# Half-width products in two chunks' scores of a graph network, and an earlier planned landing for the first gathered rows

## The chip, the cores and the metric

The kernel runs on one core of one Trainium2 chip. The metric is the device time of one execution in microseconds (us); of the kernel before, three runs are shown. The five engines of the core are named as the profile names them: PE (TensorE, with PEld for its weight loads), DVE (VectorE), ACT (ScalarE), POOL (GpSimd) and SP (SyncE, which here only issues transfers).

## What is computed

The graph has 2708 nodes with 512 features each, and a dense 0/1 adjacency matrix. Four layers follow each other, each with a residual connection and a layer norm. Layers 0, 1 and 3 are products of the adjacency with the features and a weight matrix. Layer 2, where the change lies, is two attention layers over all pairs of nodes:

```python
def _gat_layer(x, W, adj):
    proj = x @ W
    Wh, Ws = jnp.split(proj, 2, axis=-1)
    scores = Wh @ Ws.T
    a = jax.nn.softmax(scores, axis=-1) * adj
    out = a @ Wh
    out = out + x
    return jax.nn.leaky_relu(out, NEG_SLOPE)
```

The softmax runs over all 2708 nodes, and is masked by the adjacency only afterwards. So all scores are needed for the maximum and the sum, but after the mask some 16 of 2708 weights in a row are left.

## The kernel before

**Tiling.** Nodes are cut into 22 blocks of 128 (the last has 20) and, as columns, into six chunks `CH` of 512, 512, 512, 512, 384 and 276. Scores are kept turned: the score tile of block j and chunk k has block j's nodes on the partitions and chunk k's nodes in the columns.

**One attention layer** (`Attention`, from line 1385) works so. `project_steps` (line 1491) makes, for each chunk, the weights of the scores `wst` (four tiles of 128 features by the chunk's nodes) and the projected rows `z`, which go to a table `pairs` in memory. Then `layer` (line 1827) walks the chunks. For each it runs `scores` (line 1552) for blocks 0, 1, 2, 21, 3, 4 up to 20: four float32 products of 128x128 weights with 512 moving columns add up in a PSUM bank, and ACT copies the bank to a tile `s`. The hardware runs each float32 product as two instructions. Block 21, with 20 rows, puts its four products beside each other on the array (`few`, line 673), and DVE adds them up. `greatest` (line 1578) keeps the running maximum `top` of the score tiles.

**Softening.** While the scores of chunk k are made, the chunk before, k-1, is finished. `shift_rows` (line 1586) transposes `top` on PE (`tr_top`), reduces it on DVE and spreads the result, `shift_columns` (line 1607) transposes it back (`tr_mx`), and ACT copies it out. Then `soften` (line 1623) takes one block at a time: DVE subtracts the maximum, ACT takes the exponential, DVE adds to the running sum, DVE multiplies by the mask, and SP stores the block to the table `pairs`. The step of block v subtracts and exponentiates block v, and sums, masks and stores block v-1. One or two steps are recorded per block of scores. All masks of a chunk are loaded at the start of the next.

**Gathering and weighing.** When a chunk's last block is softened, `fetch` (line 1677) has POOL issue indirect transfers: each gathers, for a list of 128 neighbours, a row of the table that holds both the weights and the neighbours' `z`. Up to ten are under way. `weigh` (line 1732) multiplies such a list on PE into a bank `acc`. A block of 128 nodes takes four single lists and eight narrow ones, of which four run side by side, so a full chunk has 48 lists. There are two tables `pairs` for a layer, used in turn. `end` (line 1768) divides, adds the residual and applies the leaky relu.

**The order.** Each engine's order of instructions is that in which the program records them: `Ordered` (line 54) ties each instruction to the one before it on its engine. The program records by a clock of its own: `advance` (line 1722) adds the planned time of each product, and `weigh` takes a list when its planned landing has passed. The planned landing is set in `fetch`, lines 1697 to 1699: the lists follow each other by 1.15 us and land 6 us later, and a chunk's first begins 16 us after it is recorded. PE follows this order strictly; where a list is not there in time, it stands still. Where the walk is over, `until` and the loops behind it fill in the next layer's work (`second`, line 1902, or `early`, line 605), and `need` (line 1890) takes lists without looking at the clock where the next layer wants the rows.

**Memory.** Almost all tiles are pages of 128x512 float32 from one pool of 82; gathered lists lie in 11 wider ones. PSUM has eight banks in two halves of four: scores take theirs from half 0, transposes, sums and `acc` from half 1. `index` (line 1200) makes the lists of neighbours from marks that `note` (line 838) takes while layer 1 reads the adjacency, with tiles in a pool of its own.

Of the kernel before, what the change touches and what calls it, by code (L numbers as in the profile page):

```python
# [19 lines left out]
P = 128  # L20
# [22 lines left out]
PAGES, WIDES = 82, 11  # L43
# [44 lines left out]
class Kernel:  # L88


    def __init__(self, ctx, tc, x_in, x_t, adj, adj_t, w0, b0, w1, b1, w2, w2_t, w3, b3, out):
        self.tc, self.nc = tc, tc.nc
        nc = self.nc
        self.ctx = ctx
        self.x_in, self.x_t, self.adj, self.adj_t, self.out = x_in, x_t, adj, adj_t, out
        self.w0, self.b0, self.w1, self.b1, self.w2 = w0, b0, w1, b1, w2
        self.w2_t, self.w3, self.b3 = w2_t, w3, b3
        const = ctx.enter_context(tc.tile_pool(name="const", bufs=1))
        self.small = ctx.enter_context(tc.tile_pool(name="small", bufs=4))
        scratch = ctx.enter_context(tc.tile_pool(name="scratch", bufs=1, space=DRAM))  # L100
        tile_ = lambda name, shape, dt: const.tile(shape, dt, tag=name, name=name)
        self.ident = tile_("ident", [P, P], FP)
        self.ones = tile_("ones", [P, P], FP)
        self.ones_b = tile_("ones_b", [P, P], BF)

        self.rdeg = tile_("rdeg", [P, NB], FP)
        self.dis = tile_("dis", [P, NB], FP)
        self.nbad = len(CH) * NB
        self.bad = tile_("bad", [P, self.nbad + NB], FP)


        self.feeds = tile_("feeds", [P, NB, QUARTERS, NB], BF)
        self.givers = tile_("givers", [P, NB, LISTS], I32)

        self.base = tile_("base", [P, QUARTERS], FP)
        self.upto = tile_("upto", [P, P], BF)
        self.node = tile_("node", [P, 1], FP)
        self.block = tile_("block", [P, NB], BF)
        self.since = tile_("since", [P, P], BF)
        self.saved = [  # L120
            [scratch.tile([P, D], FP, tag=f"x{s}_{i}", name=f"x{s}_{i}") for i in range(NB)]
            for s in range(3)
        ]
        self.between = [
            scratch.tile([P, D], FP, tag=f"y_{i}", name=f"y_{i}") for i in range(NB)
        ]

        self.masks = [
            scratch.tile([P, NB, w], U8, tag=f"mask{k}", name=f"mask{k}")
            for k, (_, w) in enumerate(CH)  # L130
        ]

        self.turned = [
            [
                scratch.tile([P, DC, w], FP, tag=f"t{s}_{k}", name=f"t{s}_{k}")
                for k, (_, w) in enumerate(CH)
            ]
            for s in range(2)
        ]

    def constants(self, page):
# [4 lines left out]
        nc.gpsimd.memset(self.feeds, 0.0)  # L146
# [313 lines left out]
    def other_weights(self):  # L460


        nc = self.nc
        with self.tc.tile_pool(name="ps_bad", bufs=1, space=PSUM) as ps_bad:
            total = self.small.tile([P, 1], FP, tag="bad_sum", name="bad_sum")
            nc.vector.tensor_reduce(total, self.bad, AX.X, ALU.add)
            ps = ps_bad.tile([P, 1], FP, tag="bad", name="bad_ps")
            nc.tensor.matmul(ps, self.ones, total, start=True, stop=True)
            flag = self.small.tile([P, 1], I32, tag="flag", name="flag")
            nc.vector.tensor_scalar_min(flag, ps, 1.0)  # L470
        return nc.values_load(flag[0:1, 0:1])


def blocks_of(k):

    c0, cw = CH[k]
    return [(c0 // P + q, q * P, min(P, cw - q * P)) for q in range(-(-cw // P))]

# [37 lines left out]
class Fast:  # L516
# [4 lines left out]
    def __init__(self, kernel):  # L521
        self.k, self.tc = kernel, kernel.tc
        self.nc = Ordered(kernel.tc)
        self.notes = []
# [10 lines left out]
    def run(self):  # L535
        kernel, nc = self.k, self.nc
        with ExitStack() as ctx:
# [4 lines left out]
            self.small, self.lists = pool("small_f", 4), pool("lists", 1)  # L542
# [295 lines left out]
    def note(self, k, g, at):  # L838

        (c0, cw), (j0, j1) = CH[k], GROUPS[g]  # L840
        feeds = self.k.feeds.rearrange("p i q j -> p j (i q)")
        i0, full = c0 // QW, cw // QW
        sets = [(j0, j1, P)] if j1 < NB else [(j0, j1 - 1, P), (j1 - 1, j1, QW)]
        for q0, q1, n in ((0, full, QW), (full, -(-cw // QW), cw % QW)):
            for a, b, rows in sets if q0 < q1 else ():
                v = at[:rows, a - j0 : b - j0, q0 * QW : q0 * QW + (q1 - q0) * n]
                self.nc.vector.tensor_reduce(
                    feeds[:rows, a:b, i0 + q0 : i0 + q1],
# [351 lines left out]
    def index(self, k):  # L1200
# [8 lines left out]
        tile_ = lambda tag, shape, dt: self.lists.tile(shape, dt, tag=tag, name=f"{tag}{k}")  # L1209
# [31 lines left out]
        f = kernel.feeds[:, i0 : i0 + n, :, :]  # L1241
        nc.vector.tensor_scalar(f, f, 0.0, None, ALU.not_equal)
        some, a, b = (tile_(t, one, BF) for t in ("some", "a", "b"))
# [13 lines left out]
        kept = tile_("kept", one, BF)  # L1257
# [26 lines left out]
        def examine():  # L1284

            top = tile_("top", [P, n], FP)
# [13 lines left out]
        row, which = tile_("row", one, BF), tile_("which", one, BF)  # L1300
# [5 lines left out]
        sums = tile_("sums", [P, n, 2 * LISTS], FP)  # L1306
# [16 lines left out]
        t = tile_("list", [P, n, LISTS], FP)  # L1323
# [5 lines left out]
    def one_hot(self, s, row, which):  # L1329
# [12 lines left out]
        tile_ = lambda tag, w: self.lists.tile([P, NB, w], BF, tag=tag, name=f"{tag}{s}", bufs=2)  # L1342
        hit, both = tile_("hit", LISTS), tile_("both", 2 * LISTS)
# [13 lines left out]
class Chunk:  # L1357


    def __init__(self, ly, k):  # L1360
# [3 lines left out]
        self.s, self.masks, self.ends = {}, {}, []  # L1364
        self.softened = 0
        self.fetched, self.rden = [], None
# [12 lines left out]
class AttentionLayer:  # L1379
    def __init__(self, number, pairs):  # L1380
        self.number, self.pairs = number, pairs
        self.w, self.mixed, self.xt, self.wst = [], [], {}, {}


class Attention:
# [7 lines left out]
    def __init__(self, fast):  # L1393
# [16 lines left out]
        self.mixed = self.scratch.tile([DC, P, D], FP, tag="mixed", name="mixed")  # L1410
        self.layers = [AttentionLayer(a, self.pairs[a]) for a in range(2)]
        self.clock, self.fetch_free, self.pending = 0.0, 0.0, []

# [77 lines left out]
    def project_steps(self, ly, k):  # L1491
# [4 lines left out]
        for m in range(DC):  # L1496
# [13 lines left out]
            yield True  # L1510
        for i, lo, n in blocks_of(k):
# [29 lines left out]

    def load_moving(self, ch):
# [9 lines left out]
    def scores(self, ch, j):  # L1552
# [6 lines left out]
        if n <= QW:  # L1559
            ps = self.f.few(  # L1560
                0, name, n, cw, lambda c: wst[c][:, lo : lo + n], lambda c: ch.xt[c][:, :cw]
            )
            self.f.total(s[:n, :cw], ps, n, cw)
            self.advance(cost(cw))
# [10 lines left out]
        nc.scalar.copy(s[:n, :cw], ps[:n, :cw])  # L1575
        self.advance(DC * cost(cw))

    def greatest(self, ch, j):
        n, cw, s = rows_of(j), ch.cw, ch.s[j]
        if j == 1:  # L1580
            ch.top = self.page(f"top{ch.name}")
            self.nc.vector.tensor_max(ch.top[:, :cw], ch.s[0][:, :cw], s[:, :cw])
        elif j > 1:
            self.nc.vector.tensor_max(ch.top[:n, :cw], ch.top[:n, :cw], s[:n, :cw])
# [31 lines left out]
    def load_masks(self, ch):  # L1616
        for j0, j1 in GROUPS:
            a = self.page(f"a{ch.name}_{j0}", U8, (P, DC, ch.cw))
            self.nc.sync.dma_start(a[:, : j1 - j0, :], self.k.masks[ch.k][:, j0:j1, :])
            for j in range(j0, j1):  # L1620
                ch.masks[j] = a[:, j - j0, :]

    def soften(self, ch):
# [4 lines left out]
        if v < NB:  # L1628
            if v == 0 and ch.k >= 2:

                assert not self.chunks[ch.k - 2].to_fetch
            n = rows_of(v)
            s = ch.s[v][:n, :cw]
            nc.vector.tensor_sub(s, s, ch.shift[:n, :cw])
            nc.scalar.activation(s, s, AF.Exp)
        j = v - 1
        if j < 0:
            return
        n = rows_of(j)
# [37 lines left out]
    def fetch(self, ch):  # L1677
# [19 lines left out]
        begin = max(self.fetch_free, self.clock + (16 if (q, t) == ch.first_fetch else 0))  # L1697
# [3 lines left out]
    def load_rows(self, ch, q):  # L1701
# [7 lines left out]
        if ch.ly.number == 1:  # L1709
            ch.first[q] = self.page(f"x1{ch.name}_{q}")  # L1710
            self.nc.sync.dma_start(ch.first[q][:w], self.k.saved[1][i][:w])

    def fetch_ahead(self):
        count = sum(len(c.fetched) for c in self.chunks)
        for c in self.chunks:
            while c.to_fetch:
                if c.softened <= NB or count >= self.AHEAD:
                    return
# [13 lines left out]
    def weigh(self, wait=False):  # L1732
# [16 lines left out]
        if first:  # L1749
            ch.acc = self.bank(1, f"acc{ch.name}_{q}")  # L1750
        for h, g in enumerate(gs):
# [74 lines left out]

    def layer(self, ly, chunks, fill):
        f = self.f
        self.chunks, self.made = chunks, {}
        for k, ch in enumerate(chunks):  # L1830
            old = chunks[k - 1] if k else None


            js = [0, 1, 2, NB - 1, *range(3, NB - 1)]
            for n, j in enumerate(js):
                if old and n == 0:
                    self.load_masks(old)
                if old and n >= 3:
                    if n == 3 and k >= 3:
                        while chunks[k - 3].to_weigh:  # L1840
                            self.weigh(True)
                    for _ in range(1 + n % 2):
                        if old.softened <= NB:
                            self.soften(old)
                self.scores(ch, j)
# [3 lines left out]
                if n == 4 and k + 1 < len(chunks):  # L1849
                    self.load_moving(chunks[k + 1])  # L1850
                if k + 1 == len(chunks) and n in ((5, 11, 19) if ly.number == 0 else (5, 11)):
                    next(fill)
                if old and n == 0:
                    self.greatest(old, js[-1])
                if n:
                    self.greatest(ch, js[n - 1])
# [4 lines left out]
                if old and n == 1:  # L1861
                    self.shift_rows(old)
                if old and n == 2:
                    self.shift_columns(old)
        last = chunks[-1]
        self.load_masks(last)
        self.greatest(last, js[-1])
# [7 lines left out]

        done = self.clock + (2 if ly.number == 0 else 4)
        while last.softened <= NB:
# [108 lines left out]
```

## Time and profile before

| what | us |
|---|---|
| median of three runs | 2330.78 |
| lowest and highest run | 2322.93 to 2333.93 |
| the profiled execution: span, from its first to its last instruction | 2297.7 |
| PE busy in the span | 2269.4 |
| DVE, POOL, ACT busy | 1391.5, 705.4, 675.5 |
| scores of the first attention layer, first to last product | 760.2 to 1249.1 |
| scores of the second attention layer | 1456.2 to 1939.7 |

The profiled execution gives a span and no time of its own beside it; the difference of the median run to this span is 33.1 us. A row of a group reads: line, engine, operation, tile written, tiles read, shape and count, then the busy time and the mean of one in ns, then the idle time of the engine just before these instructions and what ended it. All instructions carry line 71, where `Ordered` issues them, so they are told apart by the names of their tiles: `sp` are the scores, `acc<-g` the products with gathered lists, `acc<-m` those of the adjacency layers. A row of the timeline reads: start, time from the first start to the last end, engine, operation, count, and in brackets the idle time before it. A row of stretches gives, behind its bounds and length, the busy time of PE, PEld, DVE, ACT and POOL with their counts, then the clock granted to PE, the busy share of the DMA engines and GB/s.

### The profile page before, as it was taken

The page shows a single profiled execution, that of the slowest core. Times are in us where ns is not written, and L with a number is a line of the kernel's source. Part 1 is how long each engine was busy: PE and PEld are TensorE (multiplying, and loading weights), DVE is VectorE, ACT ScalarE, POOL GpSimd, SP SyncE. Part 2 cuts the span into 40 slices and gives each one's busy share as a digit, 9 for nine tenths or more (in the row PEclk, how much of TensorE's full clock was granted, in tenths as well). Part 3 has the DMA queues.
Part 4 walks back from the last instruction along what each step waited for, and adds up shares of the span by engine and source line. Part 5 has one row for each costly group of instructions (what it writes and reads, how often), then busy time and mean ns, then how long its engine had stood idle before and what let it go on. Part 6 is the DMA issues. An engine that isn't in the chain of part 4 may idle for free.

```text
span 2297.7 us, 25903 instructions
## 1 busy us (share of the span) xinstructions
PE 2269.4 (99%) x8525; PEld 1289.0 (56%) x8525; DVE 1391.5 (61%) x2803; ACT 675.5 (29%) x1354; POOL 705.4 (31%) x822
## 2 busy tenths in 40 slices
PE   9999999999999999999999999999999999899997
PEld 6776876777644444443555444444443555466685
DVE  6777787786553537748667511238769788525523
ACT  7444452322111123223322200113223334342211
POOL 3433431111000001635557540001635467442000
PEclk9999999999999999999999999999999999999999
DMA  9966752223547415858789997405868799963311
GB/s 351 286 188 184 199 168 81 76 81 104 208 184 267 144 25 184 303 191 297 254 311 360 349 412 284 183 8 179 303 218 286 254 322 339 334 217 120 116 51 43
DMA packets 260929, 486.34 MB, mean 212 GB/s; under 512 B 40238, under 2 KB 126950, under 8 KB 260784
## 3 DMA queue, kind: packets, MB, share of 16 engines
q1 hardware_dynamic: 192128, 269.63, 33.6%
q0 software_dynamic: 68656, 214.96, 28.0%
q8 instruction: 69, 1.13, 0.2%
q14 instruction: 76, 0.62, 0.1%
HBM read 307.55 MB, written 176.92 MB: 211 GB/s over the span
## 4 chain that ended last, share of the span: by engine, by line
PE 86%; DMA 6%; DVE 4%; ACT 1%; issue 1%; POOL 1%; SPq 0%; ACTq 0%; POOLq 0%; DVEq 0%
PE sp L71 33%; PE acc L71 30%; PE mm L71 8%; PE z L71 6%; PE wst L71 6%; DMA x<-x 2%; DMA x<-in_x 1%; DMA at<-in_adj_t 1%; DMA g<-pairs,givers 1%; PE mix L71 1%; DMA pairs<-s 1%; POOL xt L71 1%; PE list L71 1%; ACT m L71 1%; PE tr_x2t L71 0%
## 5 line engine op out<-in xcount | busy, mean ns | idle before, releaser
L71 PE MATMUL sp<-xs,wst_sb 128*128 128x512 f32 (+3 forms) x2112 | 798.3, 544 | 0.0
L71 POOL DMA_INDIRECT g<-pairs,givers x510 | 524.2, 1028 | 872.9 <-issue 338.9
L71 PEld LDWEIGHTS sp<-xs,wst_sb 128*128 128x128 f32 (+1 forms) x2112 | 379.7, 186 | 408.4 <-issue 324.8
L71 PE MATMUL acc<-m,xh 128*128 128x512 f32 (+4 forms) x1584 | 566.8, 379 | 6.6 <-ACT m L71 5.1
L71 PE MATMUL acc<-m,xl 128*128 128x512 f32 (+4 forms) x1584 | 549.6, 365 | 2.0 <-DVE xl L71 1.8
L71 PEld LDWEIGHTS acc<-m,xh 128*128 128x128 f32 (+1 forms) x1584 | 288.0, 188 | 70.9 <-issue 21.3
L71 PEld LDWEIGHTS acc<-m,xl 128*128 128x128 f32 (+1 forms) x1584 | 288.3, 188 | 46.3 <-issue 5.3
L71 PE MATMUL acc<-g 128*32 128x512 f32 (+1 forms) x1020 | 264.8, 606 | 4.6 <-DMA g<-pairs,givers 4.0
L71 ACT COPY s<-sp 128x512 f32<-128x512 f32 (+2 forms) x252 | 132.7, 528 | 396.8 <-PE sp L71 395.1
L71 ACT ACTIVATE s<-s 128x512 f32<-128x512 f32 (+3 forms) x264 | 151.6, 580 | 319.8 <-DVE s L71 319.5
L71 DVE TENSOR_TENSOR top<-top,s 128x512 f32<-128x512 f32 (+2 forms) x240 | 149.1, 621 | 156.1 <-ACT s L71 154.5
L71 PE MATMUL mm<-w,ht 128*128 128x512 f32 (+1 forms) x528 | 223.7, 593 | 0.0
L71 ACT CAST m<-at 128x512 fp32r<-128x512 uint8 (+5 forms) x396 | 199.2, 567 | 62.3 <-DMA at<-mask 19.7
L71 DVE TENSOR_TENSOR s<-s,shift 128x512 f32<-128x512 f32 (+3 forms) x264 | 162.7, 620 | 36.2 <-ACT shift L71 36.2
L71 DVE TENSOR_TENSOR s<-s,a 128x512 f32<-128x512 f32 (+3 forms) x264 | 165.8, 628 | 13.6 <-DMA a<-mask 4.5
L71 DVE TENSOR_TENSOR sum<-sum,s 128x512 f32<-128x512 f32 (+4 forms) x252 | 156.5, 621 | 15.4 <-ACT s L71 15.4
L71 PEld LDWEIGHTS mm<-w,ht 128*128 128x128 f32 (+1 forms) x528 | 95.8, 186 | 117.0 <-issue 112.2
L71 PEld LDWEIGHTS acc<-g 128*32 128x32 f32 (+1 forms) x1020 | 74.6, 134 | 148.0 <-issue 116.5
L71 PE MATMUL z<-w,xt 128*128 128x512 f32 (+1 forms) x352 | 151.0, 596 | 0.0
L71 PE MATMUL wst<-xt,mixed 128*128 128x512 f32 (+2 forms) x384 | 150.5, 544 | 0.0
L71 POOL DMA_DIRECT2D x<-o x44 | 26.0, 597 | 329.7 <-DVE o L71 325.4
L71 PEld LDWEIGHTS wst<-xt,mixed 128*128 128x128 f32 x384 | 72.0, 190 | 71.1 <-issue 58.8
(168 smaller groups left out, 1476.7 us busy)
## 6 DMA issues: line engine op xcount, KB each, us to landing
pairs<-z_sb SPq DMA_DIRECT2D x84, 768.0 KB
pairs<-s SPq DMA_DIRECT2D x168, 256.0 KB
at<-in_adj_t SPq DMA_DIRECT2D x84, 256.0 KB
xres<-x POOLq DMA_DIRECT2D x44, 256.0 KB, 4.6
x<-o POOLq DMA_DIRECT2D x43, 256.0 KB, 3.4
pairs<-s SPq DMA_DIRECT2D x84, 128.0 KB
x<-x SPq DMA_DIRECT2D x37, 256.0 KB
at<-mask SPq DMA_DIRECT2D x32, 256.0 KB
```

The source lines that it names most:

```text
L71: ins = call(*args, **kw)
```

## The change

**Seven products for eight.** In chunks 0 and 1 of each attention layer (`SEVEN`), blocks are taken in ten pairs; blocks 18 and 21 stay alone. A pair of blocks, with the features in two halves and the columns in two halves, is a 2x2 product of quarter matrices. It took eight products of 256 columns (in the kernel before, four of 512 columns for each block, each over a quarter of the features). Winograd's form of Strassen's scheme takes seven, each over two quarters of the features, on sums of weights (s1 to s4) and of moving operands (t1 to t4). The seven are recorded interleaved over neighbouring pairs. Partial results stay in PSUM banks x and y and are copied out by ACT between additions; DVE adds what is left. The weight sums are made in `project_steps` (`sum_weights`), s3 takes the place of a quarter of the weights, which is saved to memory and restored during chunk 1, and the sums of the first four weight chunks are stored during chunk 0 and loaded again for chunk 1.

**Softening.** Subtraction, exponential and mask of a block are recorded one step apart (two in chunks 0 and 1) instead of in one or two steps. Chunks wait in a list; during chunk 1 one step is recorded at each half pair, and what is left goes on in chunk 2, with two steps a block while two chunks wait. Masks are loaded a group at a time. `shift_rows` and `shift_columns` come one block later in the walk, so between them lies block 21 and not block 2.

**The planned landing.** A chunk's first list begins 6 us of the program's clock after it is recorded, not 16.

**Beside these.** The marks of `note` and the tiles of `index` become pages, cleared a chunk at a time; the pool has 87 pages; the constant of ones becomes one column, and the final flag is summed with bfloat16 ones. The residual's second input is loaded when a block is first weighed.

```diff
-PAGES, WIDES = 82, 11
+PAGES, WIDES = 87, 11
...
+STREAMED = 4
+FIRST_LANDS = 6
+SOFT = NB + 2 * 2
+ALONE = 18
+SEVEN = [0, 1]
...
+    def sum_weights(self, ly, k):
...
+        for c in range(2):
+            nc.vector.tensor_add(tiles["s1"][c], a21[c], a22[c])
+            nc.vector.tensor_sub(tiles["s2"][c], tiles["s1"][c], a11[c])
+            nc.vector.tensor_sub(tiles["s4"][c], a12[c], tiles["s2"][c])
+            nc.sync.dma_start(self.quarter[ly.number][k][c], a21[c])
...
+    PRODUCTS = {
+        1: ("a11", "b11"),
+        2: ("a12", "b21"),
+        3: ("s4", "b22"),
+        4: ("a22", "t4"),
+        5: ("s1", "t1"),
+        6: ("s2", "t2"),
+        7: ("s3", "t3"),
+    }
+
+    def product(self, ch, t, n, out, start=False):
+
+        b, (w, x) = t["b"], self.PRODUCTS[n]
+        for c in range(2):
+            self.nc.tensor.matmul(
+                out,
+                t["sums"][w][c][:, bass.ts(b, P)],
+                ch.part[x][c],
+                start=(start and c == 0),
+                stop=(c == 1),
+                skip_group_check=not start,
+            )
+        self.advance(2 * cost(ch.half))
+
+    def pair_steps(self, ch):
...
+        def ahead(t):
+            self.product(ch, t, 2, t["y"][:, :h], start=True)
+            self.product(ch, t, 5, t["y"][:, h:cw], start=True)
+            nc.scalar.copy(t["r"][:, h:cw], t["y"][:, h:cw])
+
+        def one(t):
+            t["x"] = self.bank(t["n"] % 3 // 2, f"spx{t['name']}")[:, :h]
+            self.product(ch, t, 1, t["x"], start=True)
+            nc.scalar.copy(t["s"][:, :h], t["x"])
+
+        def six(t):
+            self.product(ch, t, 3, t["y"][:, h:cw])
+            self.product(ch, t, 6, t["x"])
+            nc.scalar.copy(t["s"][:, h:cw], t["x"])
+
+        def seven(t):
+            self.product(ch, t, 7, t["x"])
+            t["v"] = self.page(f"v{t['name']}")
+            nc.scalar.copy(t["v"][:, :h], t["x"])
+
+        def four(t):
+            self.product(ch, t, 4, t["x"])
+            nc.scalar.copy(t["r"][:, :h], t["x"])
+            ch.complete.append(t["j"][1])
+
+        def first_block(t):
+            nc.vector.tensor_add(t["s"][:, :cw], t["s"][:, :cw], t["y"][:, :cw])
+            ch.complete.append(t["j"][0])
+
+        def second_block(t):
+            nc.vector.tensor_add(t["r"][:, h:cw], t["r"][:, h:cw], t["v"][:, :h])
...
+            t = begin(n, p)
+            ahead(t)
+            if old:
+                first_block(old)
+            yield "mid"
+            one(t)
+            if older:
+                four(older)
+            if ch.k and p[1] == 0 and p[0] + 1 in groups:
+                self.load_sums(ch.ly, p[0] + 1)
...
+            yield "end"
+            if old:
+                seven(old)
+            yield "mid"
+            six(t)
+            if old:
+                second_block(old)
+            older, old = old, t
+            yield "end"
...
@@ -1626,16 +1894,23 @@
...
             nc.vector.tensor_sub(s, s, ch.shift[:n, :cw])
+        j = v - ch.apart
+        if 0 <= j < NB:
+            s = ch.s[j][: rows_of(j), :cw]
             nc.scalar.activation(s, s, AF.Exp)
-        j = v - 1
+        j -= ch.apart
         if j < 0:
             return
+        if j == NB - 1:
+            ch.softened = SOFT
...
-        begin = max(self.fetch_free, self.clock + (16 if (q, t) == ch.first_fetch else 0))
+        begin = max(self.fetch_free, self.clock + (FIRST_LANDS if (q, t) == ch.first_fetch else 0))
...
+            for what in self.walk(ch):
+                if what == "mid":
+                    self.soften_next()
+                    self.weigh()
+                    continue
+                n += 1
...
+                if old and n < 2:
+                    self.greatest(old, last=n == 1)
+                many = 2 if len(self.to_soften) > 1 else 1 + n % 2
+                for _ in range(0 if ch.seven else many):
+                    self.soften_next()
                 f.beat()
...
-                if old and n == 1:
+                if old and n == 2:
                     self.shift_rows(old)
-                if old and n == 2:
+                if old and n == 3:
                     self.shift_columns(old)
+                    self.to_soften.append(old)
```

## The prediction

> **What bounds the kernel now.** I read the page first, then the groups with their forms kept apart, then stretches of the timeline around the steps that the change moves.
>
> ```profile
> span 2297.7 us, 25903 instructions
> PE 2269.4 (99%) x8525; PEld 1289.0 (56%) x8525; DVE 1391.5 (61%) x2803; ACT 675.5 (29%) x1354; POOL 705.4 (31%) x822
> ...
> PE 86%; DMA 6%; DVE 4%; ACT 1%; issue 1%; POOL 1%; SPq 0%; ACTq 0%; POOLq 0%; DVEq 0%
> ```
>
> TensorE has work for all but 28 us of the span, and the chain that ends last is 86% TensorE. The groups by form give the scores and the vector work beside them:
>
> ```profile
> L71 PE MATMUL sp<-xs,wst_sb 128*128 128x512 f32 x1344 | 589.9, 594 | 0.0
> ```
> ```profile
> L71 DVE TENSOR_TENSOR s<-s,a 128x512 f32<-128x512 f32 x168 | 116.2, 692 | 5.8
> L71 DVE TENSOR_TENSOR s<-s,a 128x276 f32<-128x276 f32 x42 | 18.7, 446 | 5.9 <-DMA a<-mask 4.5
> ```
>
> The scores never wait (0.0 idle). Their pace is read from unbroken runs in the timeline of PE[...]:
>
> ```profile
> 1579.75 31.06 PE L71 MATMUL sp<-xs,wst_sb 128*128 128x512 f32 x72
> 1915.09 3.88 PE L71 MATMUL sp<-xs,wst_sb 128*128 128x276 f32 x16
> 916.00 0.60 PE L71 MATMUL tr_top<-ident,top 128*128 128x128 f32 x4
> ...
> 923.34 0.60 PE L71 MATMUL tr_mx<-ident,wide 128*128 128x128 f32 x4
> 1958.76 4.56 PE L71 MATMUL acc<-g 128*128 128x512 f32 x8 [0.30 <-DMA g<-pairs,givers]
> ```
>
> [...]512 columns take (31.06-0.594)/71 = 0.429 us an instruction (a product of 128 rows is two), 276 columns (3.88-0.399)/15 = 0.232. The stretches show which stage has room:
>
> ```profile
> 835.00:909.00 74.00, 74.00 (x185) 32.83 (x184) 58.40 (x93) 26.13 (x45) 4.32 (x4) 1.00 0.37 118
> 1943.00:2009.00 66.00, 55.35 (x195) 30.93 (x194) 40.45 (x92) 27.63 (x54) 34.75 (x38) 0.95 0.94 341
> ```
>
> In the second chunk's scores (835 to 909) PE is full, DVE at 79%; only the end of the second attention layer (1943 to 2009) leaves PE idle, 10.7 us, while DMA is at 0.94.
>
> [...]
>
> **Part by part.**
>
> *Seven for eight.* A pair of blocks took 2x4 products of 512 columns, 16 instructions: 6.87 us. It takes 7x2 products of 256 columns, 28 instructions. Interpolated, 256 columns cost 0.232-20x(0.429-0.232)/236 = 0.215 us[...], so 6.03 us. The weight loads, 28 for 16 at 0.190 (row of PEld), still fit under 0.215, as they do under 0.232. Saved: 0.84 us a pair, 10 pairs, 2 chunks, 2 layers: **-33.4 us**, all on the bounding engine.
>
> *What a pair adds beside it.* ACT: five half copies for two whole (about 0.36 from the 276-column copy's 0.375, against 0.58): +0.6 us, ACT then near half full. DVE: one whole and one half addition. How fast DVE goes is seen here:
>
> ```profile
> 888.32 0.69 DVE L71 TENSOR_TENSOR s<-s,shift 128x512 f32<-128x512 f32 x1
> 888.92 0.69 DVE L71 TENSOR_TENSOR sum<-sum,s 128x512 f32<-128x512 f32 x1
> 889.64 0.69 DVE L71 TENSOR_TENSOR s<-s,a 128x512 f32<-128x512 f32 x1
> 890.25 0.69 DVE L71 TENSOR_TENSOR top<-top,s 128x512 f32<-128x512 f32 x1
> ...
> 900.47 0.68 DVE L71 TENSOR_TENSOR s<-s,a 20x512 f32<-20x512 f32 x1
> ...
> 916.63 0.69 DVE L71 TENSOR_REDUCE mx<-tr_top 128x4 f32<-128x512 f32 x1 [5.99 <-PE tr_top L71]
> 917.36 0.43 DVE L71 COPY wide<-mx 128x512 f32<-128x512 f32 x1
> ```
>
> Start to start, a softened block is 1.93 us and a maximum 0.60. In chunk 1 a pair now brings two softenings (3.86), two maxima (1.2) and the additions (0.65+0.36): 6.1 us of DVE against 6.03 of PE. DVE is exactly full there, in chunk 0 not. The PSUM turns (a bank is copied out before the next product adds to it) have about 2.6 us of other products in between, against a copy of about 0.6 with its latency. Bounds: 0, as no turn need ever be late, and 1 us for each of chunk 1's 20 pairs, if each waits for a softening ahead of its addition. A gain is excluded, nothing is removed. I take **+2 us**. The sums of weights and moving operands (6 half-width DVE operations for each of 6 weight chunks, 6 for each of two score chunks, a few to replace) are about 20 us of DVE a layer, in stages where DVE is at 10 to 57%: nothing; without that cover the 20 us would come whole.
>
> *Softening moved later.* Chunk 0's 26 steps no longer end inside chunk 1: some 17 do, nine fall among the first blocks of chunk 2, with their stores (SP, where they pass the loads of the next masks, now a group at a time, and of weight sums), and the gathers on POOL behind them. Also tr_mx now follows tr_top by block 21 alone (0.9 us) instead of a whole block (3.4). Counted from the last pair's product 4 in chunk 2: PE wants tr_mx at 0.86+3.43+3.43 (blocks 1, 2)+0.44+0.9 = 9.1 us. DVE, free for it at about 1.4, has four maxima and four softenings ahead of the reduction, 10.1 us, then 0.73+0.43: 12.7. TensorE waits **3.6 us**, in both layers: **+7 us**. In chunks 3 and 5 DVE is free, and only the reduction's own 2.0 us from tr_top (916.00 to 918) shows against 1.35: 0.65 four times: **+2.6**.
>
> *First weighing earlier.* From the last softening's place in PE's order to the first product with gathered rows stood 27 us; now four to five blocks, 13.7 to 14.9. Is that enough? In the trace the place is seven blocks ahead of tr_top: 916.0-7x3.43 = 892.0. The last masked block ends at 901.2, the first gather starts at
>
> ```profile
> 903.76 1.29 POOL L71 DMA_INDIRECT g<-pairs,givers  x1 [237.77 <-issue]
> ```
>
> 11.8 us behind the place, and rows land 6.3 later (1952.4 to 1958.8 where PE stood waiting). So 18.1 for chunk 0: 4.4 too late. But by the sum above DVE catches up while PE waits for tr_mx: 11 more softening operations, 4 of block 21 and 2 maxima end at 23.4, rows land at 23.4+2.6+6.3 = 32.3, and PE gets there at 33.8. If tr_mx doesn't wait, this does; one or the other. The other chunks' first gathers stood 5.0 to 6.4 behind in layer 0 and 8.0 to 9.1 in layer 1: 11.3 to 15.4 with landing. Perhaps 0.5 in chunk 3 and 1 in chunk 5 of layer 1: **+1.5**.
>
> *The end of layer 1.* In 1957.6 to 1978.1 PE runs 16 gathered lists of chunk 4 as they land, 20.5 us for 9 us of products. The new order forces 14, whose gathers are issued earlier by two products: **-4 us**, bounds -5 and 0.
>
> *The rest* (marks of the index as pages and not a pool, the feed marks cleared on POOL a chunk at a time, the flag's product in bf16, 87 pages) issues no more work on PE and lies beside the first layers, where POOL is under half busy: nothing[...]. Some 9 MB of extra DMA a layer goes mostly into scores of chunks 0 and 1, where DMA is at 0.18 to 0.37.
>
> Sum: -33.4+2+7+2.6+1.5-4 = -24 us. The profiled span of 2297.7 becomes 2273; the 33.1 us between it and the median run, 2330.8, lie outside and stay. **2307 us.**
>
> **Rivals.** (1) *Clean saving*: the softenings' lag is taken up by slack in the banks, no new wait: 2330.8-33.4-4 = 2293. For it: PE never waited on this path before. Against: DVE's lag of 9 us at 901. (2) *DVE becomes the bound in chunk 1 and the gathers late everywhere*: 0.5 us more for each of 20 pairs, and 1 us more for each of ten first weighings: 2307+20 = 2327. For it: 6.1 against 6.03. (3) *Slower: the PSUM turns*. Each pair makes PE wait for five copies from a bank it must add to. ACT is in order, and an exponential waits for DVE's subtraction ahead of it (31 us of such waits in 835 to 909). The forecast's 24 us are gone at 24/40 = 0.6 us more a pair; at 0.4 us a turn, 2 us a pair, it is 2307+80 = 2387. Against it: 2.6 us of products between. (4) *Half instructions aren't half*: bound by something else at 0.245 us each they save nothing: 2307+33.4 = 2340. Against: 276 columns at 0.232.
>
> **How the numbers follow.** Forecast 0.62, (1) 0.15, (2) 0.13, (3) 0.06, (4) 0.04. About 0.5% (11.7 us) is what a measurement of this kernel can tell from no change. The forecast and (1) are faster: 0.77. (2) counts as the same, 0.13. (3) and (4) as slower, 0.10. The range goes from (1) to (2): 2293 to 2327, which leaves out the slower ones and a little at the ends.
>
> **What would show it.** Right: sp of 128x256 spaced 0.215; no idle of PE inside chunk 0's pairs; one wait of 3 to 4 us before tr_mx (for DVE) in chunk 2 of each layer, or else as long before the first acc<-g; about 7 us lost near the end of layer 1. Wrong: PE waiting for ACT within the pairs, acc<-g waiting on gathers in many chunks, or 256 columns well above 0.22.

## The result and the profile after

| kernel | median, us | runs | lowest to highest |
|---|---|---|---|
| before | 2324.44 | 20 | 2314.35 to 2336.58 |
| after | 2322.31 | 20 | 2315.69 to 2331.76 |

The ratio is 0.999, with a 95% interval of 0.9973 to 1.0008: no difference that can be measured. The forecast was 2307, or 0.990 of the time it started from. The profiled execution of after took 2326.53 us, with a span of 2324.8: only 1.7 us lie outside the span. So the 33.1 us that the prediction put "outside" do not exist in that form. With some 2 us outside, as every run on record has, the profiled execution of before took about 2300 us, less than the quickest of the 20 runs beside it (2314.35); in which session it was taken is not on record.

The head of the page after (span, busy time by engine, share of the chain that ended last):

```profile
span 2324.8 us, 27414 instructions
...
PE 2262.0 (97%) x9004; PEld 1387.5 (60%) x9004; DVE 1478.7 (64%) x3012; ACT 691.8 (30%) x1474; POOL 714.0 (31%) x827
...
PE 70%; DVE 10%; DMA 7%; issue 6%; ACT 2%; POOL 2%; another core or an unknown queue 1%; SPq 1%; POOLq 0%; ACTq 0%; DVEq 0%
```

PE was idle 28 us of the span before; now it is 62.8 (2324.8-2262.0). The share of PE in the chain fell from 86% to 70%: what it lost went to DVE, DMA and "issue". The half products do what the prediction says. Two of their rows in the groups by form, two turns of the timeline and the second chunk's scores as a stretch (837.8 is its first product, 903.8 the next chunk's):

```profile
L71 PE MATMUL spx<-xs,wst_sb 128*128 128x256 f32 x320 | 82.1, 380 | 1.7 <-DVE s L71 1.7
L71 PE MATMUL spy<-xs,s 128*128 128x256 f32 x128 | 33.3, 382 | 0.0
```
```profile
852.85 1.03 PE L71 MATMUL spx<-t,s 128*128 128x256 f32 x4
853.72 1.03 PE L71 MATMUL spy<-xs,wst_sb 128*128 128x256 f32 x4
```
```profile
837.80:903.80 66.00, 66.00 (x306) 55.50 (x306) 54.86 (x92) 28.57 (x68) 0.00 (x0) 1.00 0.36 110
```

Four instructions follow the last four by 0.87 us, and the median spacing of all 1120 is 0.216 (0.215 was interpolated). One wait of 1.7 us, in chunk 0, is all the idle that PSUM turns or DVE bring. PE fills its 66.0 us, and DVE, which was to be exactly full, is at 83% (90% in the second session).

So the gain was there and something took it away. The waits of PE, before:

```profile
PE acc L71 <- ACT m L71: 5.1, 3, 4.1
PE acc L71 <- DMA g<-pairs,givers: 4.0, 8, 1.2
```

and after (us in total, times, longest):

```profile
PE acc L71 <- DMA g<-pairs,givers: 17.0, 17, 5.8
PE acc L71 <- ACT m L71: 10.8, 4, 5.2
PE acc L71 <- issue: 7.7, 19, 1.1
PE tr_mx L71 <- issue: 3.3, 2, 3.1
PE wst L71 <- issue: 2.2, 1, 2.2
```

Two things are new. PE waits for gathered rows 17 us instead of 4. And it waits 13 us for nothing that the profile shows ("issue"), which before had no row for PE at all.

A third loss is in the clock column of the stretches. The first row gathered for chunk 5 of layer 0 comes late, and a stretch that begins in this wait and goes on behind it runs at half clock:

```profile
1334.89 0.64 PE L71 MATMUL den<-ones,sum 128*128 128x1 f32 x6
1341.30 2.05 PE L71 MATMUL acc<-g 128*128 128x512 f32 x2 [5.77 <-DMA g<-pairs,givers]
```
```profile
1326.00:1337.20 11.20, 9.53 (x38) 3.88 (x30) 5.43 (x12) 0.00 (x0) 3.19 (x4) 1.00 0.93 310
1337.20:1347.40 10.20, 6.11 (x7) 2.52 (x8) 0.10 (x2) 0.00 (x0) 7.76 (x9) 0.50 0.98 352
1347.40:1358.00 10.60, 10.53 (x40) 4.93 (x39) 0.00 (x0) 2.70 (x6) 3.81 (x5) 1.00 1.03 414
```

A stall of 5.8 us thus cost more than 5.8: in 10.2 us at half clock (0.50, between rows of 1.00) PE was busy for 6.1, and about half of that, some 3 us (an estimate from these two numbers), is lost again. How much slower PE works is seen in the same profile: the 512-column products `acc<-m` follow each other by 0.43 us in the half-clock stretch from 98.2 us, and by 0.23 us before and behind it. Half-clock stretches in this profile last 3.4, 6.8 or 10.2 us. The one above begins at 1337.2, 1.7 us after PE's last product had ended (1334.89+0.64). Leaving out the kernel's end, after has five such stretches, 37.5 us with PE busy for 28.1; before has one of 6.8, with 4.7. Half of the difference, (28.1-4.7)/2 = 11.7 us, is an estimate of what no row of waits contains. Only one of the five begins in a wait for gathered rows: two begin in waits for casts (`m`, 4.3 and 5.2 us), one in a wait of 3.1 us for nothing shown, one behind shorter waits.

### The profile page after: what moved, and what is told of

It reads as the page before. It is cut to its first block, busy times and chain, and to the rows that moved or that the text cites. A ratio compares the mean times of both kernels' runs of the same rounds, so it can differ in the third digit from the quotient of the medians.

```text
span 2324.8 us, 27414 instructions
## 1 busy us (share of the span) xinstructions
PE 2262.0 (97%) x9004; PEld 1387.5 (60%) x9004; DVE 1478.7 (64%) x3012; ACT 691.8 (30%) x1474; POOL 714.0 (31%) x827
## 4 chain that ended last, share of the span: by engine, by line
PE 70%; DVE 10%; DMA 7%; issue 6%; ACT 2%; POOL 2%; another core or an unknown queue 1%; SPq 1%; POOLq 0%; ACTq 0%; DVEq 0%
PE acc L71 26%; PE sp L71 12%; PE mm L71 8%; PE wst L71 6%; PE spx L71 6%; PE z L71 6%; PE spy L71 4%; DMA g<-pairs,givers 3%; DVE s L71 3%; DVE sum L71 2%; POOL g L71 1%; DMA at<-in_adj_t 1%; SPq L71 1%; DMA x<-in_x 1%
## 5 line engine op out<-in xcount | busy, mean ns | idle before, releaser
L71 POOL DMA_INDIRECT g<-pairs,givers x510 | 532.0, 1043 | 886.0 <-issue 383.4
L71 PE MATMUL acc<-m,xh 128*128 128x512 f32 (+4 forms) x1584 | 570.1, 381 | 11.4 <-ACT m L71 10.8
L71 PE MATMUL sp<-xs,wst_sb 128*128 128x512 f32 (+5 forms) x1472 | 525.1, 525 | 0.0
L71 PEld LDWEIGHTS sp<-xs,wst_sb 128*128 128x128 f32 (+1 forms) x1472 | 260.6, 185 | 252.2 <-issue 188.8
L71 PE MATMUL acc<-g 128*32 128x512 f32 (+1 forms) x1020 | 277.1, 607 | 24.5 <-DMA g<-pairs,givers 17.0
L71 ACT COPY s<-sp 128x512 f32<-128x512 f32 (+2 forms) x172 | 87.8, 511 | 488.5 <-PE sp L71 227.0
L71 DVE TENSOR_TENSOR top<-top,s 128x512 f32<-128x512 f32 (+3 forms) x240 | 149.2, 622 | 15.2 <-ACT s L71 13.0
L71 ACT ACTIVATE s<-s 128x512 f32<-128x512 f32 (+3 forms) x264 | 146.0, 579 | 33.9 <-DVE s L71 19.1
```

Source lines behind the costliest of these rows:

```text
L71: ins = call(*args, **kw)
```

## The experiments

They ran in five sessions, each on one chip, and each beside new runs of the kernel before. (In the expectations a session is named "call".) All ratios are to the kernel before of the same session, with 95% intervals. They come from all its runs, so they differ a little from the quotient of the medians; two medians of the kernel before in one session (the fifth) are 2302.41 and 2306.24. Only ratios are compared across sessions, since the kernel before itself had 2302 to 2306 us in four sessions and 2322 in the third, as it had 2324 beside the result.

**First session: take the change apart (before 2302.33).** Theory A: the seven products bring their 33 us, and the planned landing of 6 takes most of them. Rival B: the gathers bound the late stages whatever is planned. Rival C: the new order of softening is what costs.

The changed kernel with the old landing:

```diff
-FIRST_LANDS = 6
+FIRST_LANDS = 16
```


> The changed kernel, but a chunk's first list is again planned to land 16 us behind its recording. Theory A (the earlier planned landing puts products with gathered rows in PE's order ahead of their rows, and PE waits): the waits of acc<-g on gathers, 17 us in the changed kernel, fall to some 5 us, the clock is halved less often, and the time falls by 10 to 25 us, to about 2300. Theory B (gathers come at the pace of POOL and DMA whatever is planned, so the products' saving turns into waiting): the time stays within 5 us of 2322, the waits move elsewhere.

2276.08 us, ratio 0.9886 (0.9867 to 0.9906), waits for gathered rows 5.6 us. This is faster than both kernels; rival B falls.

The changed kernel without the seven products (eight, as before, and no weight sums):

```diff
-SEVEN = [0, 1]
+SEVEN = []
...
-        self.sum_weights(ly, k)
+        if SEVEN:
+            self.sum_weights(ly, k)
```


> The changed kernel with all chunks by eight products: the softening's new order and the landing of 6 us stay, the sums of weights are not made. Theory A: it pays for the landing without the saving, some 15 to 30 us above the changed kernel, 2340 to 2350. Theory B: PE was waiting for gathers anyway, so it is as fast as the changed kernel within 8 us.

2320.58 us, 1.0064 (1.0042 to 1.0085).

The kernel before with the new landing alone:

```diff
-        begin = max(self.fetch_free, self.clock + (16 if (q, t) == ch.first_fetch else 0))
+        begin = max(self.fetch_free, self.clock + (6 if (q, t) == ch.first_fetch else 0))
```


> The kernel before with nothing changed but the planned landing, 6 us for 16. Theory A: PE waits for the first rows of each chunk, 2 to 5 us at each of chunks 0 to 3, and the time rises by 10 to 25 us, to 2335 to 2350. Theory B: within 5 us of 2324.

2332.85 us, 1.0116 (1.0096 to 1.0137). One number, changed alone, costs 30.5 us. PE's waits for gathered rows:

```profile
PE acc L71 <- DMA g<-pairs,givers: 24.5, 21, 5.3
```

With eight products everywhere and the landing of 16, so that only the new order of softening and the pages are left (the softening's steps two apart in chunks 0 and 1 go with the seven products, and are gone too):

```diff
-FIRST_LANDS = 6
+FIRST_LANDS = 16
...
-SEVEN = [0, 1]
+SEVEN = []
```


> The changed kernel with all chunks by eight products and the landing of 16 us: what is left is the new order of softening, masks and transposes, and the pages. Theory C (the new order itself costs: tr_mx right behind tr_top and later gathers): 10 to 20 us above the kernel before, 2335 to 2345. Theories A and B: within 5 us of the kernel before, 2324.

2309.15 us, 1.003 (1.0022 to 1.0039). The four together: seven products 2276.08-2309.15 = -33.1 us; order of softening and pages 2309.15-2302.33 = +6.8; landing of 6, without seven products, 2320.58-2309.15 = +11.4. Theory A stands; C holds for 6.8 us, less than its range. By the intervals each of these differences from before is uncertain by 2 to 5 us. The landing costs the kernel before 30.5 us and the new order 11.4; why the new order suffers less was not separated.

Where the 6.8 us arise is seen in the traces, in the stage from chunk 4's first scores in layer 1 to the first products `mm` of the last layer: 313.7 us in this version, 308.5 to 310.5 in the three traces of the kernel before.

**Second session: first list, or all lists (before 2301.75).** The kernel after, as it is:

> The changed kernel as it is, beside three others on one chip. From its ratio of 0.999 to the kernel before, and 0.9886 for the same kernel with the first landing planned at 16 us: it should be about 24 us (1.04%) slower than that one, so ratio 0.999. If the loss were one chip's, the ratio would be near 0.989 here.

2286.17 us, 0.9933 (0.991 to 0.9956). Neither of the two: faster than before, and still some 11 us (0.0047 of 2302) above the landing of 16. The third session comes back to this.

The planned spacing of lists, at a landing of 6:

```diff
-        self.fetch_free = begin + 1.15
+        self.fetch_free = begin + 1.35
```


> The changed kernel with the planned spacing of gathered lists at 1.35 us and not 1.15; the first landing stays at 6. Theory of the first rows (only the first list of a chunk is late, by 4 to 6 us; behind it the plan holds): the spacing moves little, ratio within 0.002 of the changed kernel's 0.999. Theory of the drift (GpSimd issues a list every 1.26 to 1.4 us, so that 48 lists run 5 to 12 us behind a plan of 1.15, and the former 16 us had paid for it): most of the 24 us come back, ratio 0.990 to 0.992, and acc<-g waits for gathers fall from 17 us to under 8.

2275.34 us, 0.9876 (0.9854 to 0.9899): 10.8 us under the kernel after beside it, and level with the landing of 16. The theory of the drift holds. Why the plan drifts shows where POOL issues gathers without a pause (kernel after, second session):

```profile
2018.99 0.95 POOL L71 DMA_INDIRECT g<-pairs,givers  x1 [0.30 <-issue]
2020.25 0.95 POOL L71 DMA_INDIRECT g<-pairs,givers  x1 [0.30 <-PE acc L71]
2021.51 0.95 POOL L71 DMA_INDIRECT g<-pairs,givers  x1 [0.30 <-issue]
```

1.26 us from one to the next in these rows; over a whole chunk of this execution it is 1.38 to 1.58, but for the last (1.26). Part of that is POOL waiting for PE in its turn, but in chunk 0 of layer 1, where it waits for no product, the mean is 1.39. The plan says 1.15. A full chunk's 48 lists so fall 47x0.11 = 5.2 us behind at least, and 47x0.25 = 11.8 at 1.40. The plan carries what it believes over to the next chunk (`begin` is the later of `fetch_free` and the clock), so by the code chunk 5 starts on time in the plan and late in truth. A landing of 16 had paid for 10 us of that. The stage shows it: first scores of chunk 5 in layer 0 to the fourth chunk of projections of layer 1, in before, in after and with the spacing of 1.35:

```profile
1189.50:1390.60 201.10, 200.85 (x700) 98.28 (x699) 91.52 (x197) 42.87 (x96) 104.35 (x105) 1.00 0.99 365
```
```profile
1180.40:1392.30 211.90, 204.69 (x712) 100.51 (x711) 101.27 (x217) 42.55 (x100) 114.10 (x112) 0.98 0.98 359
```
```profile
1183.20:1386.10 202.90, 202.16 (x711) 99.44 (x710) 100.63 (x217) 43.12 (x100) 110.99 (x111) 1.00 1.02 371
```

10.8 us more in after, 1.8 with the spacing mended; in the profile of the result the same stage takes 223.9.

The landing of 16 for the last two chunks only:

```diff
-(FIRST_LANDS if (q, t) == ch.first_fetch else 0)
+((FIRST_LANDS if ch.k < 4 else 16) if (q, t) == ch.first_fetch else 0)
```


> The changed kernel with the first landing planned at 16 us for chunks 4 and 5 of each layer alone, at 6 for chunks 0 to 3. If the loss arises in the two last chunks, where the DMA engines are over 0.9 busy and the next work takes rows without looking at the plan: two thirds or more of the 24 us come back, ratio 0.989 to 0.992. If it arises evenly in every chunk: a third comes back, ratio 0.996.

2280.58 us, 0.9903 (0.9883 to 0.9923). That is 5.6 of the 10.8 us: about half lies in the last two chunks and half before, as far as intervals of 0.002 (4.6 us) tell. The ratio is in the range of the first theory, the share in neither.

The landing of 16, and `tr_mx` one block later:

```diff
-FIRST_LANDS = 6
+FIRST_LANDS = 16
...
-                if old and n == 3:
+                if old and n == (3 if ch.seven else 4):
```


> The changed kernel with the first landing planned at 16 us for all chunks, and the transposing back of the maximum (tr_mx) and the softening behind it one block later in chunks 2 to 5. If the 4.2 us of waits of tr_mx for DVE are on the path: 4 us under the version with 16 alone, ratio 0.987. If the softening, which then starts one block later, makes the first rows late: no gain or a loss of up to 5 us, ratio 0.989 to 0.991.

2279.44 us, 0.9888 (0.9865 to 0.991): no gain. The waits of `tr_mx` are gone from PE's list, others came: 8.4 us for `m` (1.5 in the version with 16 alone) and 2.8 for the load of `xt`.

**Third session: all three beside each other (before 2321.66).**

> The changed kernel once more, so that it, the first landing of 16 and the spacing of 1.35 stand on one chip. It had 0.999 on one chip and 0.993 on another. Theory of the drift of the plan: 0.993 to 0.999, and 0.5 to 1.1% above each of the two kernels beside it. If chips matter by themselves (some lose more in each stall), the place between 0.993 and 0.999 differs from chip to chip while the other two stay at 0.988.

2318.33 us over 22 runs, 0.9987 (0.9972 to 1.0001).

> The changed kernel with the first landing planned at 16 us. It had 0.9886 on another chip: 0.987 to 0.990 here, whatever the chip, since its lists are nearly always there in time.

2302.98 us, 0.9904 (0.9869 to 0.9938).

> The changed kernel with the first landing at 6 and the spacing at 1.35. It had 0.9876 on another chip. Theory of the drift: equal to the landing of 16 within 0.002. If the first rows of a chunk, too, are late (which the prediction priced at 1.5 us in all): 0.002 to 0.004 above it.

2290.01 us, 0.9864 (0.9839 to 0.9889): 0.004 under the landing of 16, which neither theory had, though the intervals overlap. The kernel after loses 28.3 us to its own version with a spacing of 1.35, where it lost 10.8 in the second session. And the kernel before with a landing of 6 and a spacing of 1.35:

> The kernel before with the first landing at 6 and the spacing at 1.35 us. With 6 alone it was 30.5 us (1.16%) slower than before. Theory of the drift: the spacing gives back most of it, ratio 0.999 to 1.003; what is left is chunk 0's first list, 4 us late in each layer. If the first rows of each chunk are the loss: ratio 1.008 or more.

2342.61 us, 1.0072 (1.0043 to 1.0101). More than expected of the drift; but its version without the spacing stood in another session.

What is different in the third session is seen in the traces. All four have rows of "issue" for PE (2.4 to 18 us) and DVE (61 to 69), as the profile of the result has; no trace of the other sessions has one for either. One such place in the profile of the result, in the timeline of ACT and then of PE and DVE:

```profile
1283.91 0.43 ACT L71 ACTIVATE s<-s 128x276 f32<-128x276 f32 x1 [0.62 <-issue]
1293.81 0.59 ACT L71 COPY mixed<-mix 128x512 f32<-128x512 f32 x1 [9.46 <-remote]
1294.29 1.08 ACT L71 ACTIVATE s<-s 128x276 f32<-128x276 f32 x3
```
```profile
1285.76 2.74 PE L71 MATMUL mix<-wt,wt 128*128 128x512 f32 x6
1294.44 1.12 PE L71 MATMUL wst<-xt,mixed 128*128 128x512 f32 x2 [2.18 <-issue]
1294.76 0.45 DVE L71 TENSOR_TENSOR sum<-sum,s 128x276 f32<-128x276 f32 x1 [7.24 <-issue]
```

ScalarE does nothing for 9.46 us. The products of `mix` that its copy needs end at 1288.50, so for 5.3 us of the 9.46 it had what it needed and stood still. Then the copy and three exponentials run without a pause. DVE's sum waits for the exponential, PE for the copy of `mixed`. In the second session the same copy came 4.81 us after ScalarE's last instruction, as soon as its products were there, and DVE went on after 2.45.

561 instructions of ScalarE in this kernel read what PE has written. In the three traces of it without such rows each starts at most 0.1 us after its products and ScalarE's instruction before it have ended. In the profile of the result 32 start over 2 us later, the longest 9.0; in that of the third session 24, the longest 9.2, 11 of them the same instructions. The other three traces of the third session have 11 to 19 such pauses.

**Fourth and fifth session: are these pauses the change's?** (before 2303.26 and 2306.24)

> The kernel before, as it is. If the call is one in which the changed kernel shows stalls for nothing that the profile shows, and these are the machine's and not the change's: TensorE 10 to 20 us and VectorE 60 to 70 us of such stalls here too, and a span of 2315 to 2330. If only the changed kernel has them: a span of 2298 to 2305 and none. In a call without them: 2298 to 2305 and none for both, and the point stays open.

2302.82 us, 1.0004 (0.9989 to 1.0018), span 2299.1, no such row.

> The kernel before with the first landing planned at 6 us. 1.0116 on another chip: 1.009 to 1.014 here.

2324.02 us, 1.011 (1.0073 to 1.0146), waits for gathered rows 21.8 us.

> The kernel before with the first landing at 6 and the lists' spacing at 1.35. It had 1.0072. Theory of the drift: at least half of what the version without the spacing loses comes back, 1.002 to 1.006. If the first list of each chunk is the loss: within 0.002 of the version without the spacing.

2310.85 us, 1.003 (1.0016 to 1.0044), waits for gathered rows 7.0 us. The spacing gives back 13.2 of 20.8 us, so the drift is the larger part here too, and the 7.6 us that remain can be those of first lists. The same code as in the third session, where 11 such pauses were found in it, is now 31.8 us quicker and without a row of "issue" for PE or DVE. It has no part of the change but the landing: the pauses are not the change's. On record the first session, without pauses, and the third, with them, also bear the same chip number, 5 (an expectation above says another chip), so the number of the chip does not tell them apart either.

> The changed kernel as it is: 0.993 and no stalls for nothing that the profile shows on TensorE and VectorE, or 0.999 and 13 to 18 us of them on TensorE. A ratio of 0.999 without such stalls, or of 0.993 with them, would refute that they set its place between the two.

2286.62 us, 0.9921 (0.9899 to 0.9943), no such row.

> The kernel before, as it is. In a call without stalls: a span of 2298 to 2305 and none on TensorE and VectorE, and the point stays open. In a call with them: 10 to 20 us on TensorE, 60 to 70 on VectorE and a span of 2315 to 2330, if they are the machine's; none and 2298 to 2305, if they are the change's.

2302.41 us, 0.9994 (0.9983 to 1.0004), no such row.

> The changed kernel as it is: a span of 2282 to 2292 without stalls for nothing that the profile shows on TensorE and VectorE, or 2308 to 2330 with 13 to 18 us of them on TensorE.

2287.18 us, 0.9921 (0.9892 to 0.995). So the kernel after stands at 0.992 to 0.993 in three sessions without such pauses (none has a row of "issue" for PE or DVE), and at 0.999 in the two with them.

## Why the prediction was wrong

| step | predicted, us | measured, us |
|---|---|---|
| seven for eight | -33.4 | -33.1 (first session) |
| PSUM turns and DVE in chunk 1 | +2 | 1.7 of waits, in chunk 0; none in chunk 1 |
| `tr_mx` in chunks 2, 3, 5 | +9.6 | 2.9 of waits; the new order and the pages cost 6.8 in all |
| first weighing earlier | +1.5 | +9 to +11; +15 to +28 with ScalarE's pauses |
| end of layer 1 | -4 | -1.2 and -1.9 in pairs of one session; +2 to +4 with the landing of 16 |
| between span and median, outside | stays | does not exist |

**Right.** The price of the half products, from 276 columns interpolated to 256: -33.1 us for -33.4, within a measurement that is not that sharp; in the stages themselves, from a chunk's first product to the next chunk's, the four changed ones lost 6.8, 8.2, 8.8 and 8.2 us, 32.0 together (the prediction's profile against that of after in the second session). A DVE addition over 256 columns takes 423 to 425 ns, where a straight line through the prediction's two rows, 692 for 512 columns and 446 for 276, gives 425. The rival of the PSUM turns is refuted by the lack of waits within the pairs, that of halves that aren't half by the spacing of 0.216.

**Not shown: "the end of layer 1: -4".** The stage from chunk 4's first scores to the last layer's first products went from 310.3 to 305.9 us in the same two traces, -4.4. But in the pairs of the fourth and the fifth session it went from 310.5 to 309.3 and from 308.5 to 306.6 only, and with the landing of 16 it takes 312.2 us with the seven products and 313.7 without, more than before.

**Near in sum, wrong in mechanism: "softening moved later".** No `tr_mx` waited 3.6 us for DVE where all engines ran on. The row of the second session:

```profile
PE tr_mx L71 <- DVE wide L71: 2.9, 6, 0.7
```

DVE's lag of 9 us at the end of chunk 1 had been read from the old order, and did not come over into the new one. Of the 6.8 us, 3 to 5 arise at the end of layer 1, where the prediction had put a gain. That the sum of this term and of the end of layer 1, +9.6-4 = +5.6, comes near the 6.8 is luck.

**The step that failed: "First weighing earlier: +1.5".** It asked, for each chunk, when its first list lands, and compared that with the four to five blocks that stand before it. Two things were left out. First, the plan runs on behind the first list: 47 more lists, planned at 1.15 us and issued at 1.26 to 1.4. The number 16 was read as the first list's margin, but it was the margin of the whole chunk. The row of 1.29 us for one gather was in the prediction, and the plan's 1.15 in the text ahead of it; the two were never set side by side. The spacing of 1.35 shows it: the first landing stays at 6, and the waits for gathered rows go from 14.8 to 6.2 us. What it does not tell apart is a list that is late within its chunk and a first list that is late because of the chunk before. Second, chunk 5 has no blocks behind it. The walk is over, PE takes layer 1's products or the lists, and the first list of layer 0 came 4.6 us late in the second session, 5.8 in the result. With the spacing of 1.35 this wait is gone too, which fits a drift carried over from chunk 4; one of 4.9 us, for the first list of chunk 4 in layer 1, stands in that trace. In the result the wait of 5.8 us, with the clock halved in and behind it (0.50 for 10.2 us), cost more than its row: 8.8 us by the estimate above.

The sum for sessions without pauses is then, by the first session alone, -33.1+6.8+11.4 = -15 us, against -15.6, -16.6 and -19.1 measured in the three others. The landing as measured in them is 10.8 by the spacing (second session), and 9 between the ratios 0.9925 and 0.9886. The sum forecast -24.

**The base: "lie outside and stay".** The 33.1 us between the profile and the median were no fixed part around the span: in a fourth-session run the kernel before had a span of 2299.1 and a time of 2301.11. In the third session its 29 runs have spans of 2308.1 to 2333.8, so what they lose lies inside the span; their mean clock, 0.994 for 0.996 elsewhere, is too little for that (0.2% is 5 us, an estimate, of some 18). ScalarE's pauses are seen in all five traces that were taken in the two sessions where the kernel before needs 2322 and more. A plan without slack seems to pay for them with late softenings, late stores and late gathers: 28.3 us between the kernel after and the same with the spacing mended, for 10.8, while the mended version keeps its ratio (0.9864 for 0.9876). This is how the change came out at nothing and not at -16, as far as the sessions show; no experiment put pauses in or took them away. That the kernel before, too, is slower there by such pauses is argued from its version with a landing of 6 and a spacing of 1.35; no trace of the kernel itself was taken in such a session. What holds ScalarE is open.

That 2322 lies inside the forecast range, near the 2327 of rival (2), is luck: of that rival the late gathers came, but DVE did not bound chunk 1, and the base was another.

A version that is better than both kernels is the changed one with the spacing of 1.35: 0.9876 and 0.9864; with the landing of 16 it is 0.9886 and 0.9904.

## What to carry to other kernels

A constant in a hand-made schedule may be paying for an error elsewhere in it: before pricing its removal, compare every planned rate with the measured one, and multiply the difference by the length of the run, not by one. Where a profile's span is well under the runs' median, look for what a slower execution does differently, and ask of the change whether it takes away the slack that absorbs it. Price a wait of the tensor engine with the clock granted in and behind it, and not with its row alone: here a row of 5.8 us came with some 3 us more.

## What the runs showed of the hardware

The profiles of before and of the result have six half-clock stretches (0.50), leaving out the kernel's end. Five began in a single wait of PE of 3.1 to 5.8 us, the sixth behind waits of 0.2 to 0.7 us; they lasted 3.4, 6.8 or 10.2 us, and one began 1.7 us after PE's last product. The mean granted clock was 0.997 for the kernel after in the second session's profile, with PE idle for 41.2 us, and 0.990 in the result's, with 62.8.

The score products of 512 columns and 128 rows in before are 672, and the trace has 1344 instructions for them. Each takes 594 ns by its own row, but they follow each other by 429 ns: they overlap. Eight instructions of narrow lists, about 0.6 us each, take 1.06 us together.

Gathers of 128 rows are issued 1.25 us apart at the least (in the profiles of before and of the result; the median is 1.26), of which 0.95 is POOL's own, and land a median 6.1 us after their issue (3.4 to 8.7, in the profile of before). In two sessions ScalarE stood still for up to 9.2 us with its products ready, 11 to 32 times over 2 us in an execution, where in three profiles of the kernel after from other sessions the longest such pause was 0.1 us; in those two, the median of the kernel before was 2322 to 2324 and not 2302 to 2306.
